# Four z columns of half B go through half A's products, with a sigmoid of their own

## The chip, the cores and the metric

The kernel runs on one core of one Trainium2 chip. The metric is device time in microseconds (us), the median of several executions; lower is better. TensorE is PE in the profile (PEld: its weight loads), VectorE is DVE, ScalarE is ACT, GpSimd is POOL, and SyncE, which issues the transfers, is SP.

## The reference

A gated recurrent layer runs over 512 time steps, for a batch of 8, with 512 inputs and 512 state units; x is added to its output.

```python
def step(h, x_t):
    fused = sigmoid(concatenate([x_t, h], axis=-1) @ w_W + w_b)
    hidden_state, output_state = split(fused, 2, axis=-1)          # r and z below
    memory_state = x_t @ wx_W + wx_b + hidden_state * (h @ wh_W + wh_b)
    h_new = output_state * h + (1.0 - output_state) * tanh(memory_state)
    return h_new, h_new
_, hs = scan(step, cond_1024, swapaxes(x, 0, 1))                   # x: (8, 512, 512), float32
return x + swapaxes(hs, 0, 1)
```

## The kernel before, in words

The 512 units lie as four chunks of 128 (k for the chunk that is contracted, j for the output's). In each output chunk the first 64 columns of a PSUM bank's parts belong to half A of the units and the others to half B. The state of half A is the contraction chunks k = 0 and 1, that of half B k = 2 and 3. Four products with j = 0 to 3 write the four groups of 32 partitions of one bank side by side.

A step needs three products of the state with weights: h (`wh_W`), z and r. They lie in three PSUM banks. Bank A has 256 columns: 64 h columns of half B, then h, z and r of half A. Bank D has 128: z, then r of half B. Bank H has the 64 h columns of half B for k = 2 and 3. `ORDER` (L27) is the order of the products in a step: A0 A1 (256 columns each), A2 A3 (192 each), D0 to D3 (128 each), H2 H3 (64 each). Each name stands for four matmuls, and each float32 matmul shows as two passes in the profile. Behind them stand products for x of later steps (`deal`, bank `xp`), three units of 96 columns in most steps, four in one of 16, and none in the last 16 steps or so. A0 and A1 need the new state of half A, A2 and A3 that of half B.

The products of x for the step ahead are copied into the three banks by ScalarE (`spread`, L310) before the step, so the banks hold complete sums. Every matmul goes through `mm` (L219), every ScalarE activation through `act` (L285), every scan through `scan` (L565).

The order of each engine's work is written out by hand (`manual_schedule`); waits between engines come from the tiles, and for PSUM from the bank that is touched. In a step, VectorE turns the r columns of half A 32 at a time (`turn_r`, L585, tile `tr`), the h columns (L594), the z columns (`turn_z`, L577, tile `tz`), and then scans for the memory state `m`, half A first. ScalarE takes the sigmoid of r (into `md0A`), the sigmoid of -z (into `hd0A`) and the tanh of `m`. A scan with `hd0A` then writes the new state `hT` (`update`). Half B follows: `turn_r_b` turns the r columns of bank D and takes their sigmoid (`md0B`), and for its z columns ScalarE takes the sigmoid first, from bank D to a tile `sz` (L626), which `turn_sz` (L631) turns afterwards into `hd0B`.

Of the kernel before, what the change touches and what calls it, by code (L numbers as in the profile page):

```python
# [7 lines left out]
F32 = mybir.dt.float32  # L8
BF16 = mybir.dt.bfloat16
AF = mybir.ActivationFunctionType  # L10
# [3 lines left out]
P = 128  # L14
NQ = 4
GS = 4
B = 8
HU = 64
# [9 lines left out]

FIRST = "A0 A1 x A2 x x A3 H0 H1 H2 H3 x D0 D1 D2 D3"

BANKS = {"A": 256, "D": 128, "H": 64}

HALF = 192

# [35 lines left out]

SC = slice(128, 512)

XP = {"A": slice(0, 256), "X": slice(256, 384), "D": slice(384, 512), "H": slice(512, 576)}


@with_exitstack
def tile_cond_rnn_residual(
# [43 lines left out]
    const = ctx.enter_context(tc.tile_pool(name="const", bufs=1))  # L121
    xin_p = ctx.enter_context(tc.tile_pool(name="xin", bufs=4))
    out_p = ctx.enter_context(tc.tile_pool(name="outp", bufs=3))
    work = ctx.enter_context(tc.tile_pool(name="work", bufs=4))
# [11 lines left out]
    def load_x(c, half=slice(0, 2), ks=slice(0, NQ)):  # L136

        if c < NCH:
            if c not in xins:
                xins[c] = xin_p.tile([P, 2, NQ, TC * B // 2], F32, tag="xin", name=f"xin_{c}")  # L140
            nc.sync.dma_start(
                out=xins[c][:, half, ks],
                in_=x[c].rearrange("p (e k n) -> p e k n", e=2, k=NQ)[:, half, ks],
            )
# [13 lines left out]
        if k == 0:  # L158
            load_x(0, 1)

    wa = const.tile([P, NQ, NQ, 256], F32, name="wa")
    for k in range(NQ):
        nc.sync.dma_start(out=wa[:, k], in_=wa_d[k])
        if k == 0:
            load_x(1, slice(0, 1))
    wd = const.tile([P, NQ, NQ, 128], F32, name="wd")
    nc.sync.dma_start(out=wd[:, :3], in_=wd_d)
    nc.sync.dma_start(out=wd[:, 3], in_=wd3_d)
    load_x(1, slice(1, 2))
# [43 lines left out]
    ctx.enter_context(tc.manual_schedule())  # L213
    whole = [{n: psum.tile([P, 512], F32, name=f"{n}{q}") for n in BANKS} for q in range(2)]
    banks = [{n: whole[q][n][:, :w] for n, w in BANKS.items()} for q in range(2)]
    xps = [psum.tile([P, 512], F32, name=f"xp{q}") for q in range(2)]

    def mm(out_, lhsT, rhs, start=False):
        nc.tensor.matmul(  # L219
            out_, lhsT, rhs, start=start, stop=False, skip_group_check=True  # L220
        )
# [62 lines left out]
    def act(key, out_, in_, func, **kw):  # L284
        inst = nc.scalar.activation(out_, in_, func, **kw).ins  # L285
        if key in written:
            tc.declare_no_dep(inst, written[key], reason="ordered through VectorE")
        written[key] = inst
        return inst
# [12 lines left out]
    def keep(g):  # L302

        nc.scalar.copy(xs[g % GS][:, SC], bank_of(g)[:, COLS])

    def source(g, c0, c1):

        return xs[g % GS][:, c0:c1] if g else xps[0][:, c0 - 64 : c1 - 64]

    def spread(g, names):  # L310

        for n in names:
            skip = 64 if n == "A" and not g else 0
            nc.scalar.copy(banks[g % 2][n][:, skip:], source(g, XP[n].start + skip, XP[n].stop))

    def turn_x(g, e):

        c0 = XP["X"].start + 32 * e
        nc.vector.transpose(md1[e // 2][g % 2][:, :, e % 2, 1 + e // 2], source(g, c0, c0 + 32))
# [10 lines left out]
    def inner_weight(n, p, j=slice(0, 2)):  # L330

        a, b = [
            (block(p, 0, 1, j), block(p, 0, 0, j)),
            (block(p, 1, 1, j), ti[:, p, 0, j]),
            (block(p, 1, 1, j), block(p, 0, 1, j)),
            (block(p, 1, 0, j), ti[:, p, 1, j]),
        ][n]
        nc.vector.tensor_tensor(ti[:, p, n, j], a, b, ALU.subtract)
# [113 lines left out]
    def take(it, n=None):  # L452
        while n is None or n > 0:
            if next(it, it) is it:
                return
            n = None if n is None else n - 1

    def x_side():
        for c in range(2, NCH):
            yield from products(c)  # L460
# [9 lines left out]
    later = x_side()  # L470
# [53 lines left out]
    for i in range(T):  # L524
        g, s = divmod(i, GS)
        c, t = divmod(i, TC)
        ps = banks[g % 2]
# [7 lines left out]
        for n in (ORDER if i else FIRST).split():  # L535
            if n == "x":
                take(first[1], 1)
                if k_ == 0:
                    keep(2)
                k_ += 1  # L540
                continue
            bank, k = n[0], int(n[1])
            hs = hT[k // 2][i % NH][:, :, k % 2, 2]
            to, w_ = {
                "A": (ps["A"], wa) if k < 2 else (ps["A"][:, 64:], wa[:, :, :, 64:]),
                "D": (ps["D"], wd),
                "H": (ps["H"], wa[:, :, :, :64]),
            }[bank]
            if bank == "A" and i == 0:
                to, w_ = xps[0][:, :HALF], wa[:, :, :, 64:]  # L550
            for j in range(NQ):
                mm(to[32 * j : 32 * j + 32, :], hs, w_[:, k, j])
        if i == 0:
# [9 lines left out]
        def scan(c_, out_, d0, d1):  # L563

            return nc.vector.tensor_tensor_scan(  # L565
                *[t_[:, :, c_].rearrange("p n c s -> p (n c s)") for t_ in (out_, d0, d1)],
                0.0,
                ALU.mult,
                ALU.add,
            ).ins  # L570

        pa = ps["A"][:, HU:] if i else xps[0][:, :HALF]
        raw = {"h": (pa[:, :HU], ps["H"]), "z": (pa[:, HU : 2 * HU],), "r": (pa[:, 2 * HU :], ps["D"][:, HU:])}

        def turned(n, hf):
            t_ = work.tile([P, 2, 32], F32, tag=f"t{n}{hf}", name=f"t{n}{hf}_{i}")
            inst = nc.vector.transpose(t_.rearrange("p c n -> p (c n)"), raw[n][hf]).ins  # L577
            return t_[:, :, rows], inst
# [5 lines left out]
        def turn_r(q):  # L584
            nc.vector.transpose(tr[:, q], raw["r"][0][:, 32 * q : 32 * q + 32])  # L585
            act(
                ("r", 0, q, g % 2, s),
                md0[0][g % 2][:, rows, q : q + 1, 1].rearrange("p n c -> p c n"),
                tr[:, q : q + 1, rows],
                AF.Sigmoid,  # L590
            )

        def turn_h(hf):
            inst = nc.vector.transpose(  # L594
                md1[hf][g % 2][:, :, :, hf].rearrange("p n c -> p c n"), raw["h"][hf]
            ).ins
            h_done[hf] = inst
            if hf == 0 and i + 1 - NH in pool_done:
                tc.add_manual_dep(inst, pool_done[i + 1 - NH].name, SYNC)
# [16 lines left out]
        def turn_r_b():  # L616
            t_, _ = turned("r", 1)
            for q in range(2):
                act(
                    ("r", 1, q, g % 2, s),  # L620
                    md0[1][g % 2][:, rows, q : q + 1, 2].rearrange("p n c -> p c n"),
                    t_[:, q : q + 1],
                    AF.Sigmoid,
                )
            sz = work.tile([P, HU], F32, tag="sz", name=f"sz_{i}")
            act(("sz", i % 4), sz, ps["D"][:, :HU], AF.Sigmoid, scale=-1.0)  # L626
            return sz

        def turn_sz(sz):
            done = [  # L630
                nc.vector.transpose(hd0[1][i % 2][:, :, q, 2], sz[:, 32 * q : 32 * q + 32]).ins  # L631
                for q in range(2)
            ]
            mark = nc.vector.memset(idle[:, IDLE - 3 : IDLE - 2], 0.0).ins
            tc.add_manual_dep(mark, done[0].name, SYNC)
# [9 lines left out]
        def memory(hf, q):  # L645

            c_ = slice(q, q + 1)
            scan(c_, ms[hf], md0[hf][g % 2][:, rows], md1[hf][g % 2][:, rows])
            act(("n", hf, q, i % NH), state(hf, i, 1)[:, :, c_], ms[hf][:, :, c_, 1 + hf], AF.Tanh)

        def update(hf, q):
            new = hT[hf][(i + 1) % NH][:, B * s1 : B * s1 + B]
            z_ = hd0[hf][i % 2][:, rows] if hf else hd0[hf][i % 2]
            return scan(slice(q, q + 1), new, z_, hT[hf][i % NH][:, rows])

        turn_r(0)
        turn_h(0)
        turn_r(1)
# [5 lines left out]
        if i == 0:  # L664
            for p in (3, 4):
                inner_weight(0, p)
        sz = turn_r_b()
        update(0, 0)
        turn_h(1)
        update(0, 1)  # L670
# [5 lines left out]
        if i == T - 1:  # L676
# [4 lines left out]
                ALU.add,  # L681
            )
        memory(1, 1)
        turn_sz(sz)
        update(1, 0)
        update(1, 1)
        for hf in range(2):
# [130 lines left out]
```

## Time and the profile before

| | before |
|---|---|
| median of 3 runs | 1625.81 us (1625.53 to 1626.62) |
| profiled execution | 1626.4 us, span 1624.6 us |
| PE busy, share of the span | 1613.8 us, 99% |
| PEld busy | 1311.1 us, 81% |
| DVE busy | 1414.4 us, 87% |
| ACT busy | 1092.7 us, 67% |
| granted TensorE clock | 1.0 |

The profiled execution lies 1.8 us above its own span and 0.6 us above the median of the runs. Matmuls are pipelined in the records: each one's duration holds its way through the array, so a busy PE isn't PE at its peak, and waits are better read from where weight loads and products start. Of the views, the timeline lists instructions in order of time (start, length, engine, line, what is written and read, count, and in brackets the idle time before and what ended it), the groups list mean durations by shape, and the waits sum who waited for whom.

### The profile page before, as it was taken

To read this page: it belongs to the slowest core of one execution; us is meant where nothing else is said; L and a number is where in the kernel's file an instruction comes from. 1 tells how busy PE (TensorE), PEld (TensorE's weight loads), DVE (VectorE), ACT (ScalarE), POOL (GpSimd) and SP (SyncE) were. 2 spreads that over 40 slices of the span, in tenths; PEclk is the share of its full clock that TensorE was granted. 3 is DMA by queue.
4 is the path that set the end of the run, shared out by engine and by line. 5 is a ranking of instruction groups with operands and counts; after the bars stand their busy time and mean duration, and the time that the engine had idled before them with its cause. 6 is when DMAs were issued, how large, how long until landed. Compare 5 with 4: busy or idle time off the path is not lost.

```text
span 1624.6 us, 121051 instructions
## 1 busy us (share of the span) xinstructions
PE 1613.8 (99%) x49211; PEld 1311.1 (81%) x49211; DVE 1414.4 (87%) x12269; ACT 1092.7 (67%) x6545; POOL 539.7 (33%) x1443
## 2 busy tenths in 40 slices
PE   9999999999999999999999999999999999999998
PEld 6888888888888888888888888888888888888876
DVE  8988888888888888888888888888888888888887
ACT  4766666666666666666666666666666666666666
POOL 2223333333333333333333333333333333333321
PEclk9999999999999999999999999999999999999999
DMA  5011111111111111111111111111111111111110
GB/s 192 12 40 33 29 37 38 43 32 31 33 42 40 35 33 32 39 39 38 35 29 37 38 43 32 30 34 42 40 34 35 31 39 38 38 35 24 31 35 10
DMA packets 66225, 62.10 MB, mean 38 GB/s; under 512 B 9856, under 2 KB 64000, under 8 KB 65664
## 3 DMA queue, kind: packets, MB, share of 16 engines
q1 hardware_dynamic: 65664, 54.35, 12.8%
q8 instruction: 385, 6.31, 1.6%
q14 instruction: 176, 1.44, 0.3%
HBM read 14.96 MB, written 8.39 MB: 14 GB/s over the span
## 4 chain that ended last, share of the span: by engine, by line
PE 98%; DVE 1%; DMA 0%; issue 0%; SPq 0%; ACT 0%
PE A L219 49%; PE D L219 27%; PE xp L219 16%; PE H L219 7%; DMA wx<-in_wx_dram 0%; DVE tr L585 0%; DVE md1B L638 0%; DVE tr L577 0%; DVE md1A L594 0%; DVE tz L577 0%; DVE hT L565 0%; DVE m L565 0%; SPq L132 0%; ACT hT L285 0%; DVE hd0B L631 0%
## 5 line engine op out<-in xcount | busy, mean ns | idle before, releaser
L219 PE MATMUL A<-wa,hT 128*32 128x256 f32 x16352 | 875.8, 354 | 3.8 <-DVE hT L565 3.8
L219 PEld LDWEIGHTS A<-wa,hT 128*32 128x32 f32 x16352 | 500.5, 123 | 256.5 <-DVE hT L565 132.9
L219 PE MATMUL D<-wd,hT 128*32 128x128 f32 x16384 | 541.1, 273 | 0.0
L219 PEld LDWEIGHTS D<-wd,hT 128*32 128x32 f32 x16384 | 480.7, 122 | 21.4 <-issue 0.3
L734 POOL TENSOR_TENSOR ot<-xin,hT 128x32 f32<-128x32 f32 x503 | 135.1, 269 | 1043.1 <-DVE hT L565 1025.5
L285 ACT ACTIVATE md0A<-tr 128x8 f32<-128x8 f32 x1024 | 215.7, 211 | 375.9 <-DVE tr L585 366.9
L285 ACT ACTIVATE hT<-m 128x8 f32<-128x8 f32 x2048 | 380.7, 210 | 46.1 <-DVE m L565 0.2
L585 DVE STREAM_TRANSPOSE tr<-A 128x32 f32<-128x32 f32 x1022 | 199.6, 195 | 198.8 <-PE A L219 197.8
L285 ACT ACTIVATE hT<-hT 128x16 f32<-128x16 f32 x1024 | 232.1, 227 | 92.5 <-DVE hT L565 91.1
L219 PE MATMUL H<-wa,hT 128*32 128x64 f32 x8208 | 208.4, 219 | 0.0
L219 PEld LDWEIGHTS H<-wa,hT 128*32 128x32 f32 x8208 | 185.8, 122 | 0.0
L565 DVE TENSOR_TENSOR_SCAN hT<-hd0B,hT 128x24 f32<-128x24 f32 x1024 | 172.0, 208 | 1.4 <-DVE hT L565 1.4
L565 DVE TENSOR_TENSOR_SCAN m<-md0A,md1A 128x16 f32<-128x16 f32 x1024 | 172.0, 168 | 0.0
L565 DVE TENSOR_TENSOR_SCAN hT<-hd0A,hT 128x24 f32<-128x24 f32 x1024 | 169.5, 166 | 0.0
L285 ACT ACTIVATE md0B<-tr 128x8 f32<-128x8 f32 x1024 | 159.9, 206 | 1.1 <-DVE tr L577 1.1
L565 DVE TENSOR_TENSOR_SCAN m<-md0B,md1B 128x24 f32<-128x24 f32 x1024 | 154.5, 192 | 0.0
L631 DVE STREAM_TRANSPOSE hd0B<-sz 128x32 f32<-128x32 f32 x1024 | 148.9, 190 | 0.0
L219 PE MATMUL xp<-ti,si 128*32 128x192 f32 (+1 forms) x3120 | 146.8, 295 | 0.0
L450 POOL TENSOR_TENSOR xs<-ff 128x192 f32<-128x192 f32 x240 | 139.8, 599 | 0.1
L638 DVE STREAM_TRANSPOSE md1B<-A 128x64 f32<-128x64 f32 x511 | 133.1, 260 | 0.0
L577 DVE STREAM_TRANSPOSE tr<-D 128x64 f32<-128x64 f32 x512 | 127.8, 250 | 0.1
L594 DVE STREAM_TRANSPOSE md1B<-H 128x64 f32<-128x64 f32 x512 | 127.3, 249 | 0.0
(110 smaller groups left out, 1855.6 us busy)
## 6 DMA issues: line engine op xcount, KB each, us to landing
ff<-tt SPq DMA_DIRECT2D x120, 96.0 KB, 2.4
ff<-tt SPq DMA_DIRECT2D x120, 72.0 KB, 2.5
out_dram<-ot SPq DMA_DIRECT2D x128, 64.0 KB, 1.8
xin<-in_x_dram SPq DMA_DIRECT2D x112, 64.0 KB, 2.1
ff<-ff SPq DMA_DIRECT2D x60, 96.0 KB, 2.1
ff<-ff SPq DMA_DIRECT2D x60, 72.0 KB, 2.7
wx<-in_wx_dram SPq DMA_DIRECT2D x4, 768.0 KB, 8.3
wa<-in_wa_dram SPq DMA_DIRECT2D x4, 512.0 KB, 10.6
```

Of the source, the lines that this page charges most:

```text
L219: nc.tensor.matmul(out_, lhsT, rhs, start=start, stop=False, skip_group_check=True)
L285: inst = nc.scalar.activation(out_, in_, func, **kw).ins
L450: nc.gpsimd.tensor_tensor(to, a, b, ALU.add)
L565: return nc.vector.tensor_tensor_scan(*[t_[:, :, c_].rearrange("p n c s -> p (n c s)") for t_ in (out_, d0, d1)], 0.0, ALU.mult, ALU.add,).ins
L577: inst = nc.vector.transpose(t_.rearrange("p c n -> p (c n)"), raw[n][hf]).ins
L585: nc.vector.transpose(tr[:, q], raw["r"][0][:, 32 * q : 32 * q + 32])
L594: inst = nc.vector.transpose(md1[hf][g % 2][:, :, :, hf].rearrange("p n c -> p c n"), raw["h"][hf]).ins
L631: nc.vector.transpose(hd0[1][i % 2][:, :, q, 2], sz[:, 32 * q : 32 * q + 32]).ins
L638: nc.vector.transpose(md1[1][g % 2][:, :, :, 0].rearrange("p n c -> p c n"), ps["A"][:, :HU])
L734: pool_done[i + 1] = nc.gpsimd.tensor_tensor(ot[:, t], x_of(c, slice(0, NQ), t, 1), hTs[(i + 1) % NH][:, :, :, B * s1 : B * s1 + B, 2].rea ...
```

## The change

`EARLY = 4`. Bank A grows from 256 to 260 columns, and its last four are the first four z columns of half B. Bank D shrinks from 128 to 124. The products of k = 2 and 3 into bank A grow from 192 to 196. In each step ScalarE gets one more activation: the sigmoid of those four columns, from bank A to the first four columns of `sz`, written ahead of `turn_r(0)`. The later one takes 60 columns of bank D in place of 64. The weights, the bias and the columns of x are laid out to fit. No other instruction is added or taken away.

```diff
-BANKS = {"A": 256, "D": 128, "H": 64}
+EARLY = 4
+BANKS = {"A": 256 + EARLY, "D": 128 - EARLY, "H": 64}
...
-            to, w_ = xps[0][:, :HALF], wa[:, :, :, 64:]
+            to, w_ = xps[0][:, : HALF + EARLY], wa[:, :, :, 64:]
...
-        pa = ps["A"][:, HU:] if i else xps[0][:, :HALF]
-        raw = {"h": (pa[:, :HU], ps["H"]), "z": (pa[:, HU : 2 * HU],), "r": (pa[:, 2 * HU :], ps["D"][:, HU:])}
+        pa = ps["A"][:, HU:] if i else xps[0][:, : HALF + EARLY]
+        raw = {
+            "h": (pa[:, :HU], ps["H"]),
+            "z": (pa[:, HU : 2 * HU],),
+            "r": (pa[:, 2 * HU : 3 * HU], ps["D"][:, HU - EARLY :]),
+        }
...
-            sz = work.tile([P, HU], F32, tag="sz", name=f"sz_{i}")
-            act(("sz", i % 4), sz, ps["D"][:, :HU], AF.Sigmoid, scale=-1.0)
-            return sz
-
-        def turn_sz(sz):
+            act(("sz", i % 4), sz[:, EARLY:], ps["D"][:, : HU - EARLY], AF.Sigmoid, scale=-1.0)
+
+        def turn_sz():
...
+        sz = work.tile([P, HU], F32, tag="sz", name=f"sz_{i}")
+        act(("sz early", i % 4), sz[:, :EARLY], pa[:, 3 * HU :], AF.Sigmoid, scale=-1.0)
         turn_r(0)
         turn_h(0)
         turn_r(1)
...
-        sz = turn_r_b()
+        turn_r_b()
...
-        turn_sz(sz)
+        turn_sz()
...
-    wa_d = chunks(cat((whm, half_b), (whm, half_a), (z[D:], half_a), (r[D:], half_a)))
-    wd = units(cat((z[D:], half_b), (r[D:], half_b)))
+    wa_d = chunks(cat((whm, half_b), (whm, half_a), (z[D:], half_a), (r[D:], half_a), (z[D:], early)))
+    wd = units(cat((z[D:], later), (r[D:], half_b)))
```

ScalarE's order at step 240, before. `md0A` and `md0B` are the sigmoids of r of the two halves, `hd0A` that of half A's z, `sz` that of half B's z, and `hT<-m` is a tanh; numbers behind a name tell tiles and steps apart, and the brackets say for which engine's count an instruction waits.

```order
L314 COPY H_171<-xs_163 128x64
L285 ACTIVATE md0A_98<-tr_240_23203 128x8 [waits DVE_49] x2
L285 ACTIVATE hd0A_106<-tz_240_23211 128x16 [waits DVE_49]
L285 ACTIVATE hT_90<-m_240_23204 128x8 [waits DVE_49] x2
L285 ACTIVATE md0B_100<-tr_240_23220 128x8 [waits DVE_49]
L285 ACTIVATE md0B_100<-tr_240_23220 128x8
L285 ACTIVATE sz_23224<-D_170 128x64 [waits PE_49,Activation_49]
```

The same place in the changed kernel, whose lines are numbered some 7 to 11 higher:

```order
L321 COPY H_171<-xs_163 128x64
L292 ACTIVATE sz_23446<-A_169 128x4 [waits PE_49,Activation_49]
L292 ACTIVATE md0A_98<-tr_240_23443 128x8 [waits DVE_49] x2
L292 ACTIVATE hd0A_106<-tz_240_23453 128x16 [waits DVE_49]
L292 ACTIVATE hT_90<-m_240_23444 128x8 [waits DVE_49] x2
L292 ACTIVATE md0B_100<-tr_240_23462 128x8 [waits DVE_49]
L292 ACTIVATE md0B_100<-tr_240_23462 128x8
L292 ACTIVATE sz_23446<-D_170 128x60 [waits PE_49,Activation_49]
```

One activation of 4 columns is new ahead of the first `md0A`, and it waits for TensorE.

VectorE's order at the start of step 240, before (`idle` marks filler writes that end the step ahead):

```order
L713 MEMSET idle 128x1 x2
L585 STREAM_TRANSPOSE tr_240_23203<-A_169 128x32 [waits PE_49]
L594 STREAM_TRANSPOSE md1A_102<-A_169 128x64
L585 STREAM_TRANSPOSE tr_240_23203<-A_169 128x32
L577 STREAM_TRANSPOSE tz_240_23211<-A_169 128x64
```

And in the changed kernel:

```order
L724 MEMSET idle 128x1 x2
L596 STREAM_TRANSPOSE tr_240_23443<-A_169 128x32 [waits Activation_49]
L605 STREAM_TRANSPOSE md1A_102<-A_169 128x64
L596 STREAM_TRANSPOSE tr_240_23443<-A_169 128x32
L588 STREAM_TRANSPOSE tz_240_23453<-A_169 128x64
```

VectorE's instructions keep their order; the first transposition of a step waited for TensorE before, and waits for ScalarE now.

More of the change, by code (lines that the diff above doesn't have):

```diff
@@ L71 @@
 SC = slice(128, 512)
-XP = {"A": slice(0, 256), "X": slice(256, 384), "D": slice(384, 512), "H": slice(512, 576)}
+XP = {
+    "A": slice(0, 256 + EARLY),
+    "X": slice(256 + EARLY, 384 + EARLY),
+    "D": slice(384 + EARLY, 512),
+    "H": slice(512, 576),
+}
 @with_exitstack
@@ L159, in tile_cond_rnn_residual @@
             load_x(0, 1)
-    wa = const.tile([P, NQ, NQ, 256], F32, name="wa")
+    wa = const.tile([P, NQ, NQ, BANKS["A"]], F32, name="wa")
     for k in range(NQ):
@@ L165, in tile_cond_rnn_residual @@
             load_x(1, slice(0, 1))
-    wd = const.tile([P, NQ, NQ, 128], F32, name="wd")
+    wd = const.tile([P, NQ, NQ, BANKS["D"]], F32, name="wd")
     nc.sync.dma_start(out=wd[:, :3], in_=wd_d)
@@ L570, in scan @@
             ).ins
-        pa = ps["A"][:, HU:] if i else xps[0][:, :HALF]
-        raw = {"h": (pa[:, :HU], ps["H"]), "z": (pa[:, HU : 2 * HU],), "r": (pa[:, 2 * HU :], ps["D"][:, HU:])}
+        pa = ps["A"][:, HU:] if i else xps[0][:, : HALF + EARLY]
[3 more added lines that the diff above has]
+            "r": (pa[:, 2 * HU : 3 * HU], ps["D"][:, HU - EARLY :]),
+        }
         def turned(n, hf):
@@ L780 @@
     half_a, half_b, both = slice(0, 64), slice(64, 128), slice(0, 128)
+    early, later = slice(64, 64 + EARLY), slice(64 + EARLY, 128)
     r, z = w[:, :512], w[:, 512:]
@@ L785, in chunks @@
         return c_(units(a).swapaxes(0, 1))
-    wx_d = chunks(cat((z[:D], half_a), (r[:D], half_a), (wxm, both), (z[:D], half_b), (r[:D], half_b)))
-    wa_d = chunks(cat((whm, half_b), (whm, half_a), (z[D:], half_a), (r[D:], half_a)))
-    wd = units(cat((z[D:], half_b), (r[D:], half_b)))
+    wx_d = chunks(
+        cat((z[:D], half_a), (r[:D], half_a), (z[:D], early), (wxm, both), (z[:D], later), (r[:D], half_b))
+    )
+    wa_d = chunks(cat((whm, half_b), (whm, half_a), (z[D:], half_a), (r[D:], half_a), (z[D:], early)))
+    wd = units(cat((z[D:], later), (r[D:], half_b)))
     wd_d, wd3_d = c_(wd[:, :3]), c_(wd[:, 3])
@@ L792 @@
     bias_d = (
-        cat((whb, half_a), (zb, half_a), (rb, half_a), (wxb, both), (zb, half_b), (rb, half_b), (whb, half_b))[0]
+        cat(
+            (whb, half_a),
+            (zb, half_a),
+            (rb, half_a),
+            (zb, early),
+            (wxb, both),
+            (zb, later),
+            (rb, half_b),
+            (whb, half_b),
+        )[0]
     )
```

## Prediction

> **What bounds the kernel now.** I read the page's totals first, then the chain of waits, then one step in the timeline, and last a stretch that lacks part of the work.
>
> ```profile
> PE 1613.8 (99%) x49211; PEld 1311.1 (81%) x49211; DVE 1414.4 (87%) x12269; ACT 1092.7 (67%) x6545; POOL 539.7 (33%) x1443
> PE 98%; DVE 1%; DMA 0%; issue 0%; SPq 0%; ACT 0%
> ```
>
> Both lines name TensorE: busy for 99% and 98% of the chain. That alone would say that only matmul columns count, and the change keeps their number. So the question is whether the other engines really have room. A step from the middle, cut to the rows that matter:
>
> ```profile
> 802.70 0.65 PEld L219 LDWEIGHTS A<-wa,hT 128*32 128x32 f32 x16
> 802.77 1.71 PE L219 MATMUL A<-wa,hT 128*32 128x256 f32 x32
> ...
> 803.34 0.33 DVE L565 TENSOR_TENSOR_SCAN hT<-hd0B,hT 128x24 f32<-128x24 f32 x2
> ...
> 803.60 0.51 PEld L219 LDWEIGHTS A<-wa,hT 128*32 128x32 f32 x16 [0.26 <-DVE hT L565]
> ...
> 804.30 1.06 PE L219 MATMUL D<-wd,hT 128*32 128x128 f32 x32
> 804.55 0.22 DVE L585 STREAM_TRANSPOSE tr<-A 128x32 f32<-128x32 f32 x1 [0.25 <-PE A L219]
> 804.80 0.44 ACT L285 ACTIVATE md0A<-tr 128x8 f32<-128x8 f32 x2 [0.58 <-DVE tr L585]
> 805.06 0.18 DVE L565 TENSOR_TENSOR_SCAN m<-md0A,md1A 128x16 f32<-128x16 f32 x1
> 805.31 0.15 DVE L565 TENSOR_TENSOR_SCAN m<-md0A,md1A 128x16 f32<-128x16 f32 x1
> 805.39 0.67 PE L219 MATMUL xp<-ti,si 128*32 128x192 f32 x16
> 805.42 0.25 DVE L577 STREAM_TRANSPOSE tr<-D 128x64 f32<-128x64 f32 x1
> 805.59 0.17 DVE L565 TENSOR_TENSOR_SCAN hT<-hd0A,hT 128x24 f32<-128x24 f32 x1
> 805.81 0.21 PEld L219 LDWEIGHTS A<-wa,hT 128*32 128x32 f32 x8
> 805.88 0.40 PE L219 MATMUL A<-wa,hT 128*32 128x256 f32 x4
> ```
>
> The step lasts 805.88 - 802.77 = 3.11 us. It is a loop: the A products end at 802.77 + 1.71 = 804.48, VectorE begins to turn them at 804.55, ScalarE takes sigmoids, the scan at 805.59 ends at 805.76 with half A's first new state, and at 805.81, 0.05 later, the next A0 loads it as weights, 0.07 ahead of its first matmul. Half B's state is as late: its two scans run from 803.34 to 803.67, behind the first of them its weights begin to load at 803.60, and the loader had waited 0.26 for them. So each new state arrives at about the moment in which TensorE gets to it. How much room is that? The end of the run tells, since the last steps have no products for x:
>
> ```profile
> 1571.32 1.77 PE L219 MATMUL A<-wa,hT 128*32 128x256 f32 x32 [0.24 <-DVE hT L565]
> ...
> 1617.90 1.43 PE L219 MATMUL A<-wa,hT 128*32 128x256 f32 x21 [0.23 <-DVE hT L565]
> ```
>
> TensorE idles there for 0.23 to 0.24 in each step, yet 15 steps take 46.58 us, 3.105 each. The loop through the two half states takes that by itself, with TensorE mostly waiting for it. Over the whole run:
>
> ```profile
> 23.39 1.99 PE L219 MATMUL A<-wa,hT 128*32 128x256 f32 x32
> ...
> 815.23 1.71 PE L219 MATMUL A<-wa,hT 128*32 128x256 f32 x32
> 818.50 1.70 PE L219 MATMUL A<-wa,hT 128*32 128x256 f32 x32
> ```
>
> From this first full step to the one at 1617.90 are 510 steps in 1594.51 us, 3.1265 each (the average holds the steps with a fourth unit of x, such as the one of 3.27 from 815.23 to 818.50). TensorE's work and the loop are level, within some 0.02 us. Whatever is put in series into the loop is paid nearly in full, 510 times.
>
> **The change part by part.** These rows carry the prices (groups by shape: count, busy us, mean ns):
>
> ```profile
> L219 PE MATMUL D<-wd,hT 128*32 128x128 f32 x16384 | 541.1, 273 | 0.0
> L219 PE MATMUL A<-wa,hT 128*32 128x256 f32 x8176 | 535.5, 379 | 3.8 <-DVE hT L565 3.8
> L285 ACT ACTIVATE md0A<-tr 128x8 f32<-128x8 f32 x1024 | 215.7, 211 | 375.9 <-DVE tr L585 366.9
> L285 ACT ACTIVATE sz<-D 128x64 f32<-128x64 f32 x512 | 104.4, 204 | 0.0
> L314 ACT COPY D<-xs 128x128 f32<-128x128 f32 x127 | 33.6, 265 | 0.1
> L189 ACT ACTIVATE table<-zeros 128x1 f32<-128x1 f32 x1 | 0.2, 203 | 0.0
> L314 ACT COPY D<-xp 128x128 f32<-128x128 f32 x1 | 0.3, 258 | 0.0
> L314 ACT COPY H<-xp 128x64 f32<-128x64 f32 x1 | 0.2, 197 | 9.6 <-PE xp L219 9.6
> DVE tr L585 <- PE A L219: 197.8, 492, 0.9
> ```
>
> *Matmul widths.* A column costs (379 - 273) / 128 = 0.83 ns in a pass. Four of them in the eight passes of A0 to A3 (the four j run side by side) put the end of A 27 ns later, and D's eight passes take them back: D3, H and x end where they did. TensorE's sum is unchanged, but the loop, which runs through all of A, gets 27 ns longer.
>
> *The end of D.* Relative to A's end, D now ends 27 ns earlier. `tr<-D` started 0.06 after D's end (804.30 + 1.06 = 805.36; 805.42), as the first `tr` did 0.07 after A's, so D's end does release it. But VectorE only finished the scan of 805.31 at 805.46 and overlaps its instructions by a few hundredths, so it could not start much sooner: I take 10 ns as gained, of the 27. Another 10 ns go at A2, which gets its weights a little earlier relative to the wider A1.
>
> *The new activation and the new wait.* This is the term that decides. The early sigmoid can't start before A's end. In the order of the section on the change, VectorE's first `tr`, released by TensorE before, now waits for that activation: both read bank A. So it starts one ScalarE operation and one handover later. Nothing else hides the delay: VectorE sat idle ahead of this very instruction in 492 of the steps, 0.40 us in the mean (the waits row above), and behind it are queued all the transpositions and scans of both halves, whose ScalarE work waits for them in turn. The trace has no activation of 4 columns. From below: copies out of PSUM take 258 ns for 128 columns and 197 for 64, so a straight line gives about 140 for 4; I take 150. From above: 1 column took 203, 8 columns 211, and 64 columns of the very same kind, `sz`, 204. Those small ones don't follow the line, and are nearest in size, so I take 190. The handover from ScalarE to VectorE is 805.06 - (804.80 + 0.21) = 0.05, with 0.03 (`tr` to `md0A`: 804.55 + 0.22 to 804.80) and 0.08 as its ends. ScalarE hears of TensorE about as soon as VectorE does, at most 0.01 sooner. The term is 0.19 + 0.05 - 0.01 = 0.23 us, between 0.18 and 0.29.
>
> The Trainium skill prices this differently ("ScalarE: Activation LUTs", "What ACT_TABLE_LOAD costs"): 186 ns plus 0.833 ns a column with immediate operands, 93 ns more for a pointer operand, hence 189 or 282 ns here as an estimate. For `sz` the same rule gives 239 or 332, and the trace has 204, so it errs high. With 189 the sum stays; with 282 it would be near 1781.
>
> *The late sigmoid* has 60 columns in place of 64, 3 ns, and VectorE reaches it behind other work. ScalarE's busy share rises by 512 x 0.19 = 97 us, to (1092.7 + 97) / 1734 = 69%, and costs nothing by itself. `spread` copies four columns more and four fewer.
>
> *Sum.* A step takes 3.105 (the loop alone) + 0.027 - 0.020 + 0.23 = 3.342, which is above TensorE's own work even in the steps with four units of x. Against 3.1265 that is 0.2155 x 510 = 110 us. In the 20 steps or so in which VectorE was busy up to the first `tr`, part of the delay is hidden: 2 us off. From 1626.4 of the profiled execution this gives 1734; the runs' median lies 0.6 below that execution, which is less than I can resolve. I say 1735.
>
> By the ends: 0.18 with both gains gives 3.292, +84 us less 2, 1708; 0.29 without them gives 3.422, +151, 1775.
>
> **The rivals.** *Faster.* The end of D, not the wait, decides. Against the loop of 3.11 in a middle step, D's earlier end would give back 10 to 13 ns a step, 5 to 7 us: 1620. For it speaks that D's end releases `tr<-D`. It decides only if the first `tr` is delayed by less than some 10 ns, so the activation would have to be over when the A products end, and it reads their result. 0.04.
>
> *No change.* The delay disappears under the products for x, as the 98% suggest: 1626. Against it, without those products a step still took 3.105, so they cover only what the loop leaves over, some 0.02. 0.03.
>
> *Dearer.* The early sigmoid costs as much as a 128-column copy, 265 ns, since it begins cold on a bank just written. Then the term is 0.305, the step 3.417, and the run 1626.4 + 148 - 2 = 1772. For it speaks nothing but that no row has this shape behind such a wait. The skill's dearer price, above, lies on this side. 0.07.
>
> That the change doesn't do what it says I leave out: the rows of its order show it.
>
> **How the numbers follow.** The forecast gets 0.86. About 0.2% (3 us) is what a measurement of this kernel can tell from no change. Slower is forecast and dearer together, 0.93; same 0.03; faster 0.04. The range runs from the lower end, 1708, to the upper one, 1775, which holds the dearer case; the two small rivals are left out.
>
> **What the changed profile would show.** The early `sz<-A` of 150 to 210 ns, starting 0.06 to 0.07 after the A products; the first `tr` waiting for it, and not for PE; steps of 3.34 us; TensorE idle ahead of A0 by about 0.2 us in every step, where it had been only in the last ones; PE's busy share down to about 93% (3.11 of 3.342); `tr<-D` no longer starting 0.06 after D's end but behind the scan ahead of it. I'm wrong if the first `tr` still starts 0.07 after A's end, if the steps stay at 3.11 to 3.13, or if TensorE doesn't idle although the states come later.

## The result

The changed kernel takes 1722.76 us (median of 5 runs, 1722.42 to 1723.50) against 1626.29 for the kernel before in the same comparison: 1.0594 times as long, 95% interval 1.0579 to 1.0610. That is 96.5 us or 0.19 us a step. The forecast was 1735, slower, in a range from 1708 to 1775.

### The profile page after: what moved, and what is told of

It is laid out like the page before. It is cut to its first block, busy times and chain, and to the rows that moved or that the text cites. A ratio compares the mean times of both kernels' runs of the same rounds, so it can differ in the third digit from the quotient of the medians.

```text
span 1720.7 us, 121810 instructions
## 1 busy us (share of the span) xinstructions
PE 1705.8 (99%) x49211; PEld 1289.5 (75%) x49211; DVE 1399.1 (81%) x12269; ACT 1145.7 (67%) x7057; POOL 538.1 (31%) x1443
## 4 chain that ended last, share of the span: by engine, by line
PE 97%; DVE 2%; ACT 1%; issue 0%; ACTq 0%; DVEq 0%
PE A L226 52%; PE D L226 24%; PE xp L226 15%; PE H L226 7%; DVE tr L596 0%; DVE md1B L647 0%; ACT sz L292 0%; DVE hT L572 0%; DVE tr L588 0%; DVE md1A L605 0%; DVE tz L588 0%; DVE m L572 0%; ACT hT L292 0%; ACT md0A L292 0%; ACT xs L311 0%
## 5 line engine op out<-in xcount | busy, mean ns | idle before, releaser
L226 PE MATMUL A<-wa,hT 128*32 128x260 f32 x16352 | 912.9, 363 | 9.2 <-DVE hT L572 7.6
L226 PEld LDWEIGHTS A<-wa,hT 128*32 128x32 f32 x16352 | 483.4, 125 | 370.2 <-DVE hT L572 270.9
L226 PE MATMUL D<-wd,hT 128*32 128x124 f32 x16384 | 527.2, 269 | 0.0
L226 PEld LDWEIGHTS D<-wd,hT 128*32 128x32 f32 x16384 | 469.5, 122 | 25.5 <-DMA wd<-in_wd_dram 0.5
L292 ACT ACTIVATE sz<-A 128x4 f32<-128x4 f32 x511 | 89.1, 174 | 245.8 <-PE A L226 241.3
L572 DVE TENSOR_TENSOR_SCAN hT<-hd0A,hT 128x24 f32<-128x24 f32 x1024 | 188.3, 184 | 0.0
```

The source lines that it names most:

```text
L226: nc.tensor.matmul(out_, lhsT, rhs, start=start, stop=False, skip_group_check=True)
L572: return nc.vector.tensor_tensor_scan(*[t_[:, :, c_].rearrange("p n c s -> p (n c s)") for t_ in (out_, d0, d1)], 0.0, ALU.mult, ALU.add,).ins
```

## The profile after

The page first, busy time and the chain of waits:

```profile
PE 1705.8 (99%) x49211; PEld 1289.5 (75%) x49211; DVE 1399.1 (81%) x12269; ACT 1145.7 (67%) x7057; POOL 538.1 (31%) x1443
PE 97%; DVE 2%; ACT 1%; issue 0%; ACTq 0%; DVEq 0%
```

TensorE still shows 99%, in a run that is 6% longer with the same matmuls. The loader's share fell from 81% to 75%, VectorE's from 87% to 81%. The waits say why (who waited for whom: total us, times, longest). The first row is of the kernel before, the others are of the changed one:

```profile
PEld A L219 <- DVE hT L565: 132.9, 499, 0.5
...
DVE tr L596 <- ACT sz L292: 312.8, 507, 1.6
PEld A L226 <- DVE hT L572: 270.9, 1020, 0.7
ACT sz L292 <- PE A L226: 241.3, 474, 0.8
```

VectorE's first transposition waits for the early sigmoid, 0.62 us in the mean where it had waited 0.40 for TensorE. The weight loads of bank A wait for the new state 1020 times, two times a step, where it had been 499: half A's state is late now as well as half B's. A step in the timeline, cut:

```profile
821.77 1.78 PE L226 MATMUL A<-wa,hT 128*32 128x260 f32 x32
...
823.62 0.17 ACT L292 ACTIVATE sz<-A 128x4 f32<-128x4 f32 x1 [0.33 <-PE A L226]
823.83 0.22 DVE L596 STREAM_TRANSPOSE tr<-A 128x32 f32<-128x32 f32 x1 [0.60 <-ACT sz L292]
...
824.44 0.67 PE L226 MATMUL xp<-ti,si 128*32 128x192 f32 x16
...
824.66 0.23 DVE L588 STREAM_TRANSPOSE tr<-D 128x64 f32<-128x64 f32 x1
824.81 0.20 DVE L572 TENSOR_TENSOR_SCAN hT<-hd0A,hT 128x24 f32<-128x24 f32 x1
...
825.06 0.62 PEld L226 LDWEIGHTS A<-wa,hT 128*32 128x32 f32 x16 [0.16 <-DVE hT L572]
```

The A products end at 823.55, ScalarE begins at 823.62, VectorE at 823.83: 0.28 after the products, where it had been 0.07. The next A0 comes at 825.06, 3.29 after the last. The x products' records reach to 824.44 + 0.67 = 825.11 and cover the gap ahead of A0: only the loader's 0.16 shows it. In the last steps, without x, the gap is plain, 0.44 where it was 0.24:

```profile
22.09 2.00 PE L226 MATMUL A<-wa,hT 128*32 128x260 f32 x32
...
1664.00 1.79 PE L226 MATMUL A<-wa,hT 128*32 128x260 f32 x32 [0.44 <-DVE hT L572]
...
1713.68 1.78 PE L226 MATMUL A<-wa,hT 128*32 128x260 f32 x32 [0.44 <-DVE hT L572]
```

From the first to the last of these rows are 510 steps of 3.317 us; the last 15, from 1664.00, take 3.312 each. With and without x products a step lasts nearly the same: the loop alone sets it.

## The experiments

Three theories: W, the wait of VectorE's first transposition for the early activation is the price; P, the wider A products are; S, one more activation on ScalarE is.

**The layout alone.**

```diff
-        act(("sz early", i % 4), sz[:, :EARLY], pa[:, 3 * HU :], AF.Sigmoid, scale=-1.0)
...
-            act(("sz", i % 4), sz[:, EARLY:], ps["D"][:, : HU - EARLY], AF.Sigmoid, scale=-1.0)
+            act(("sz", i % 4), sz, ps["D"][:, :HU], AF.Sigmoid, scale=-1.0)
```

> The changed kernel with its wider A and narrower D, but without the early activation: the late sigmoid takes 64 columns of bank D again, so four units of each chunk get a wrong z (that part of the computation is left out). Theory W (the wait of VectorE's first transposition for the early activation is the whole price): the products alone cost nothing, TensorE's own work of about 3.10 us a step is the floor, 1615 to 1627 us. Theory P (the longer A products, which lie in the loop, are the price): most of the 96 us stay, 1700 or more. Theory S (one more activation on ScalarE is the price, wherever it stands): like W here.

1620.49 us, 0.9963 of the kernel before (0.9949 to 0.9976): a little faster, with the sigmoid of four columns left out. P as the main price falls. Waits and timeline:

```profile
DVE tr L596 <- PE A L226: 204.7, 495, 0.9
805.26 1.72 PE L226 MATMUL A<-wa,hT 128*32 128x260 f32 x32
...
807.05 0.22 DVE L596 STREAM_TRANSPOSE tr<-A 128x32 f32<-128x32 f32 x1 [0.30 <-PE A L226]
...
807.90 0.25 DVE L588 STREAM_TRANSPOSE tr<-D 128x64 f32<-128x64 f32 x1
...
808.36 0.84 PE L226 MATMUL A<-wa,hT 128*32 128x260 f32 x12
```

A step takes 3.10. `tr<-D` comes 0.85 behind the first `tr`, where it was 0.87: the earlier end of D is worth that here. In the mean of 460 steps the gain behind `tr` is 0.026 and the A products take 0.016 more (1.728 for 1.712), so a step is some 0.01 shorter. The layout thus has a gain of its own of 6 us, and the early sigmoid costs 1722.8 - 1620.5 = 102.

**The wait alone, on the kernel before.**

```diff
+        spare = work.tile([P, 4], F32, tag="spare", name=f"spare_{i}")
+        act(("spare", i % 4), spare, pa[:, 2 * HU : 2 * HU + 4], AF.Sigmoid, scale=-1.0)
         turn_r(0)
```

> The kernel before, with one activation more in each step: 4 columns of bank A into a tile that nobody reads, at the place of the early sigmoid. Widths unchanged. W: the same wait, without the 17 ns by which the A products got longer, so steps of about 3.30 and 1705 to 1722 us. P: 1626. S: 1705 to 1722 too.

1714.98 us, 1.0545 (1.0530 to 1.0559): 88.5 of the 96.5 us, without any other width. Groups, waits and timeline:

```profile
L285 ACT ACTIVATE spare<-A 128x4 f32<-128x4 f32 x511 | 88.6, 173 | 239.9 <-PE A L219 235.5
DVE tr L585 <- ACT spare L285: 307.4, 507, 1.7
...
823.56 0.22 DVE L585 STREAM_TRANSPOSE tr<-A 128x32 f32<-128x32 f32 x1 [0.48 <-ACT spare L285]
...
824.40 0.23 DVE L577 STREAM_TRANSPOSE tr<-D 128x64 f32<-128x64 f32 x1
```

`tr<-D` comes 0.84 behind `tr` here too, although D is as long as before: once the first `tr` is late, D's end no longer releases anything. `tr<-D` starts 0.25 behind it in the mean, where it had been 0.07. This is why the layout's gain is gone in the changed kernel, and its longer A remains: 1722.8 - 1715.0 = 8 us.

**The same activation without the wait.** It reads 4 columns of the bias in SBUF (`bias[:, :4]`) in place of bank A.

> The kernel before, with one activation more in each step at the same place, which reads 4 columns of the bias in SBUF in place of bank A, so that neither ScalarE nor VectorE waits for anything new. W: 1624 to 1630 us, no change. S: 1700 or more, since ScalarE's work is the same as with the early sigmoid. P: 1626.

1626.95 us, 1.0001 (0.9992 to 1.0010).

```profile
L285 ACT ACTIVATE spare<-head 128x4 f32<-128x4 f32 x512 | 99.8, 195 | 0.0
DVE tr L585 <- PE A L219: 198.4, 493, 0.9
```

ScalarE's new activations take 100 us, more than the 89 of the early sigmoid, and cost nothing. S falls; W stands. The two kernels differ in what the activation reads, and so in when it runs. From SBUF it waits for nothing and starts 0.48 us before the A products end, in the mean. From bank A it starts behind them, and VectorE, which reads the bank next, waits for it. A ScalarE that is taken up at just that moment isn't the price either: in the wait alone the activation is over 0.24 behind the products (0.07 + 0.173), and in the kernel before ScalarE's next work, `md0A`, began only 0.32 behind them (804.80 - 804.48). The Trainium skill ("PSUM — Partial Sum Buffer", "PSUM bank collisions raise a hardware error") says that the compiler's scheduler puts instructions of two engines in order if they touch one bank in the same 32 partitions, even where both only read. These two runs agree: the first `tr` waits for the activation 507 times in one and for TensorE 493 times in the other, with 88 us between them. What the chip would do without that order wasn't tried.

**A longer activation.** As in the wait alone, over 128 columns (`pa[:, :128]`).

> The kernel before with an idle activation ahead of VectorE's first transposition as in read_a, but over 128 columns of bank A in place of 4. W: the activation takes about 0.26 us in place of 0.174, so each step is some 0.085 longer than there: 1715 + 511 x 0.085 = 1758 us, 1750 to 1765. If VectorE only waited for something that ends with the products (a handover, not the activation's length): 1715, unchanged.

1765.79 us, 1.0863 (1.0845 to 1.0881). What reads and writes the tile:

```profile
L285 ACT ACTIVATE spare<-A x511: 275/277/285, 24.9 to 1758.8; 128x128 f32<-128x128 f32 x171
  DVE tr L585: 360.4, 511
```

The activation takes 277 ns, not 260. It is 104 longer than the one of 4 columns, 53 us in 511 steps; the run is 50.8 longer (51.8 if each run is taken from the kernel before of its own comparison, 1626.5 and 1625.5). The wait is paid at nearly its full length. My range for this run, up to 1765, missed by under 1.

**The fourth step.** In the changed kernel the early sigmoid starts late in one step of four:

```profile
828.36 1.79 PE L226 MATMUL A<-wa,hT 128*32 128x260 f32 x32
830.27 0.17 ACT L292 ACTIVATE sz<-A 128x4 f32<-128x4 f32 x1 [0.56 <-PE A L226]
```

It is 0.12 behind the products, not 0.07. These are the steps whose row in the order has two waits, for TensorE and for ScalarE's own copy into the bank some steps before, long done. The section on the change names no instruction beyond the activation, but in the trace 126 of the 511 early activations have an instruction of ScalarE's own ahead of them that does nothing but wait. The experiment hands the second one to a state copy that waits for nothing:

```diff
+            if hf == 0 and s == GS - 1 and (g + 1, "A") in copied:
+                tc.add_manual_dep(inst, copied[g + 1, "A"].name, SYNC)
```

> The changed kernel, in which the early activation of every fourth step no longer waits for an earlier copy of ScalarE besides TensorE: a copy of the state, which waits for nothing, takes over that second wait some steps ahead of it. In the changed kernel the early activation starts 128 ns after the A products in every fourth step and 67 in the others. Theory V (the second wait, though long met, is an instruction of its own and costs 61 ns): 67 ns in all steps, 127 x 0.061 = 7.8 us less, 1715 us. Rival (the fourth step is late for another reason, such as the copies of x into the next banks): 1722 to 1723, unchanged.

1712.28 us, 1.0535 (1.0520 to 1.0551), 10.5 less than the changed kernel (9.7 if each is taken from the kernel before of its own comparison), where 7.8 were expected. The same kind of step:

```profile
824.00 1.78 PE L226 MATMUL A<-wa,hT 128*32 128x260 f32 x32
825.84 0.17 ACT L293 ACTIVATE sz<-A 128x4 f32<-128x4 f32 x1 [0.49 <-PE A L226]
```

0.06 behind the products. A second wait costs some 0.06 us, even where it has long been met, if it stands on the loop. The 2 to 3 us beyond the 7.8 I can't assign.

**The early sigmoid out of the way.** It moves behind half A's second tanh, when VectorE has done with bank A:

```diff
-        act(("sz early", i % 4), sz[:, :EARLY], pa[:, 3 * HU :], AF.Sigmoid, scale=-1.0)
         turn_r(0)
...
+        act(("sz early", i % 4), sz[:, :EARLY], pa[:, 3 * HU :], AF.Sigmoid, scale=-1.0)
         turn_r_b()
```

> The changed kernel with the early activation moved behind half A's second tanh, ahead of half B's sigmoids of r, where VectorE has done with bank A: the same work, and VectorE's first transposition is released by TensorE again. W: 1615 to 1640 us, near the kernel before, the upper end if the activation pushes half B's sigmoids back by about 0.03. S: 1700 or more, since ScalarE has as much to do. P: 1700 or more.

1639.73 us, 1.0080 (1.0067 to 1.0092): 83 us of the loss are back, by place alone. It is still 13 slower than before and 19 slower than the layout alone.

```profile
L292 ACT ACTIVATE sz<-A 128x4 f32<-128x4 f32 x511 | 79.3, 155 | 0.1
PEld A L226 <- DVE hT L572: 99.5, 480, 0.5
PEld A L226 <- ACT sz L292: 27.2, 133, 0.5
```

The last row is new: A0 writes bank A, so it now waits for the early sigmoid too, besides the state. Two steps of this run show what that costs, the first with both waits, the second with the state's alone:

```profile
805.61 0.17 DVE L572 TENSOR_TENSOR_SCAN hT<-hd0A,hT 128x24 f32<-128x24 f32 x1
805.66 0.15 ACT L292 ACTIVATE sz<-A 128x4 f32<-128x4 f32 x1
...
805.89 0.66 PEld L226 LDWEIGHTS A<-wa,hT 128*32 128x32 f32 x16 [0.19 <-ACT sz L292]
...
815.07 0.17 DVE L572 TENSOR_TENSOR_SCAN hT<-hd0A,hT 128x24 f32<-128x24 f32 x1
815.11 0.15 ACT L292 ACTIVATE sz<-A 128x4 f32<-128x4 f32 x1
...
815.29 0.66 PEld L226 LDWEIGHTS A<-wa,hT 128*32 128x32 f32 x16
```

In the first, A0's weights begin to load 0.11 behind the scan that writes half A's state, in the second 0.05. The second is one step of four, in which the products turn to the other set of banks, which the sigmoid hasn't just read. In the median of 460 steps the load begins 0.116 behind the scan in three steps of four, and 0.054 behind it in the fourth; with the layout alone it is 0.054 in both kinds. The 0.116 stays the same whether the sigmoid ends 0.028 or 0.043 behind the scan. So it isn't the sigmoid's end that delays A0 but the second wait itself, by 0.06 like the activation above; the trace has 383 instructions more of the loader's own that do nothing but wait (480 against 97). Steps that end in an A0 with both waits are 0.045 to 0.053 longer than with the layout alone, and those with one wait 0.004: together that makes the 19 us. The run lies just inside the range of W, but not for the reason given there: half B's sigmoids of r still begin 0.03 behind `tr<-D`.

**The same, with one wait for A0.** The activation goes between half A's two tanhs, the x products behind it in the program, and the last of these takes the wait:

```diff
+        one = act(("sz early", i % 4), sz[:, :EARLY], pa[:, 3 * HU :], AF.Sigmoid, scale=-1.0)
+        if i > PLAIN[-1]:
+            before = last_mm[0]
+            deal(later, 4 if (i + LEAD) % TC == TC - 1 else 3)
+            if last_mm[0] is not before:
+                tc.add_manual_dep(last_mm[0], one.name, SYNC)
```

> The changed kernel with the early activation between half A's two tanhs, after VectorE's last reading of bank A; the products of x stand behind it in the program, and the last of them waits for it, so that the next A0 has one wait again as before. The second wait of every fourth step is moved as in one_wait. W with TensorE's floor of 3.10 us a step: 1616 to 1626 us, a little faster than the kernel before, as with the layout alone (1620). If the wait of the last product of x, or the two waits of the activation itself, bite: 1630 to 1650.

1662.21 us, 1.0227 (1.0212 to 1.0242): worse than either guess.

```profile
822.17 0.40 PE L228 MATMUL A<-wa,hT 128*32 128x260 f32 x3
822.20 0.25 PE L228 MATMUL xp<-ti,si 128*32 128x96 f32 x1
822.28 1.70 PE L228 MATMUL A<-wa,hT 128*32 128x260 f32 x29
```

The second wait is gone from A0: its weights begin to load 0.054 behind the scan again, in the median. But the four products of a group no longer run side by side: three groups of partitions are in A0 while the fourth is still at its x product. The A products now take 1.87 in the mean, where the layout alone takes 1.73. That the wait on the last product of a group of four sets the four apart is my reading of these rows; the run also moved the x products in the program, and no run separates the two. No version with the whole computation was faster than the kernel before; the most that any of these runs gained is the 6 us of the layout alone.

## Why the prediction was right

The sign, the place and the mechanism held: the first `tr` waits for the early sigmoid, and with the loop level with TensorE's work, every step pays. Term by term, in us a step:

| term | predicted | measured |
|---|---|---|
| early activation | 0.190 | 0.174 |
| handover to VectorE | 0.05 | 0.033 (mean; 823.62 + 0.174 to 823.83 in the step above) |
| ScalarE hears sooner than VectorE | -0.01 | 0 (0.07 both) |
| wider A, less what A2 wins back | 0.027 - 0.010 | 0.014 (1.772 to 1.785 in the last 15 steps) |
| from the first `tr` to the next A0 (put down to D's end) | -0.010 | -0.030 (1.266 to 1.236 there) |
| second wait in every fourth step | not seen | 0.015 (0.06 / 4) |
| a step | 3.342 | 3.317 (3.312 in the last 15 steps) |

From 3.105, the measured terms add up to 3.311.

The rows of the activation, from the changed kernel's groups:

```profile
L292 ACT ACTIVATE sz<-A 128x4 f32<-128x4 f32 x511 | 89.1, 174 | 245.8 <-PE A L226 241.3
```

The 0.025 too much, times 510, is the 12 us by which 1735 was high. It is a balance of misses in both directions: the activation (0.016), the handover (0.017) and the gain behind `tr` (0.020) made the forecast too high, the second wait, which I hadn't seen, (0.015) and ScalarE's head start (0.010) too low. That they partly cancel is luck. I took the activation from rows of the same size and passed over the line through the copies; the truth lies between. The Trainium skill's price in "ScalarE: Activation LUTs", "What ACT_TABLE_LOAD costs", comes near with immediate operands: it gives 189 ns for 4 columns and 293 for 128 as estimates, against 174 and 277 here, the same slope and 15 or 16 too much. By its dearer price, for a pointer operand, 4 columns would take 282 as an estimate, and no run here shows that. Which kind of operand the activation has, the profile doesn't say.

The end of D was sized too small as a gain and for the wrong reason: I let it move `tr<-D` by 0.01, but the layout alone shows 0.02 to 0.03, while in the changed kernel the late `tr` alone does it: `tr<-D` comes 0.83 behind `tr` there, and 0.84 with the old D as well. The rival in which D's end decides was thus true of the layout, -6 us, and was outweighed as its condition said.

One sign named ahead failed. TensorE's share did not fall to 93%: the records of the x products are long enough to cover the gap. I had noted that a busy PE isn't PE at its peak, and used it as a marker all the same; the loader's waits were the better one. ScalarE's share, put at 69%, came out at 67%: busy time counts overlapping rows once, and it grew by 53 us and not by the 89 of the new activations.

## What to carry to other kernels

Where a chain through several engines returns as often as the busiest engine frees itself, room is measured by a stretch that lacks part of that engine's work, not by its busy share. An operation that is cheap on an idle engine is dear if a busier engine must wait for it: ask which bank or tile it touches, who touches that next, and put it after them. A wait that is moved onto an instruction with a wait of its own isn't free, even if it is met in time: it cost 0.06 us each time here. When an experiment moves a wait away, look at who gets it.

## What was not expected of the hardware

- A second wait delayed an instruction by 0.06 us though it was met in time: an activation in the changed kernel (0.12 behind the products in place of 0.06), and a weight load with the early sigmoid out of the way (0.116 behind the scan in place of 0.054).
- The same 4-column activation takes 174 ns from idle, behind a wait, and 155 right behind another activation.
- With a wait on one of four side-by-side products, three of A0's began at 822.17, ahead of the fourth product of x at 822.20.
